# A graph attention layer's feed-forward with tanh in place of Silu, its last step on VectorE, and roots read two places later

## The chip, the cores and the metric

The kernel runs on one core of a Trainium2 chip. A core has a matrix engine (TensorE, PE in the profile), three engines for elementwise work (VectorE or DVE, ScalarE or ACT, GpSimd or POOL) and SyncE (SP), which issues DMAs. Each engine works through its own instructions in order; semaphores hold one back until another engine or a DMA has delivered. The metric is the device time of one execution in microseconds (us). The kernel before takes 10435.46 us, the median of three runs (10427.23 to 10443.66).

## The reference

Two graph layers on 10000 nodes with 512 features and 160000 edges sorted by their target node, each followed by a residual sum and a normalisation. The first layer is a mixture of four graph convolutions of two steps each, of which two are chosen per node. The second is attention along the edges with eight heads of 64, then a feed-forward part, which is what the change touches:

```
z = layernorm(x)
q, k, v = z @ Wq.T, z @ Wk.T, z @ Wv.T             (split into 8 heads)
s = sum(q[src] * k[dst]) / sqrt(64) + att_bias     (per edge and head)
alpha = softmax of s over the edges of one node
x = x + (sum of alpha * v[dst]) @ Wo.T + bo
z = layernorm(x)
x = x + silu(z @ W1.T + b1) @ W2.T + b2            (W1: 1024 x 512)
```

silu(v) is v times the logistic function of v, which equals (v/2) (1 + tanh(v/2)). The layer's own residual and one more normalisation end the computation. All data are 32-bit floats.

## The kernel before

Nodes are taken in 79 blocks of 128, and a block in four windows of 32 nodes. The edges of a window lie in up to five chunks of 128 (`CAP`). `fast` runs through four stages. First the edges are sorted into slots, interleaved with the first convolution step. The second convolution step follows, block by block, with the residual, two normalisations by `normed` (L721) and the projections to q, k and v, which go to memory. These stages are held together by TensorE's order.

The last stage is attention and feed-forward, over 316 windows. Its order on TensorE, VectorE, ScalarE and POOL is written out by hand (`manual_schedule`): each engine receives its instructions in the order in which the Python loop over `w` issues them. In each window:

- POOL gathers keys and values of the edges by indirect DMA, two windows ahead (`pull`, L1397, into four buffers `kvb`).
- TensorE turns the one-hot edge matrices (L1406), ScalarE copies them out of PSUM (L1409), and TensorE expands the queries to the edges in three groups (`expand`, L1610, into two PSUM buffers `qe`).
- VectorE multiplies expanded queries by keys, one instruction per group (`score`, L1624), and reduces over each head (L1651).
- `weigh` makes weights out of scores, in steps that are spread over three windows: per-head maxima (L1519), turned by TensorE (L1521), reduced again (`top`, L1524), spread (L1526) and subtracted (L1528); the exponential on ScalarE (L1531), with a check against very low scores (`far`, L1533); weights times one-hot matrices, in part on POOL, in part on VectorE (`ohp`, L1540); the weighted sum of the values on TensorE (`sums`, L1554); the division by the denominator (`den`, L1559 and L1560; `att`, L1563); and the turned result, copied to `att_t` (L1566).

Output projection, normalisations and feed-forward are filled in between these as jobs. A job is a Python generator: it issues instructions and yields a cost. `advance(rate)` is called four times per window, in two of them with a credit (2.6 and 2.4), and goes once through the list of jobs. A job that has yielded 0 takes one step per call; a positive cost is a step of TensorE, which is issued while the credit lasts. So a `yield 0` puts the rest of a job one place (about a quarter of a window) later.

- `front(b)`: output projection of a block (L1423), residual (L1429), statistics (L1432) and `scale`, normalised rows on ScalarE (L1435), turned (L1446) and copied to `z_t` (L1447). Two blocks share one `z_t`.
- `back`: for two blocks, the eight pieces `f` of the hidden layer. Each piece takes four products of TensorE into one half of a PSUM bank (L1464), then Silu on ScalarE, which writes `hid` (L1466). Piece f + 2 uses the same half bank as f. Then, for each block, eight down products (L1473).
- `tail`: residual (L1481), statistics (L1485), `scale`, the result `o` on ScalarE (L1488) and its store (L1490).
- `scale`: aggregate on VectorE (L1502); the root on ScalarE (L1505); one place later reciprocal and product on VectorE (L1507, L1508). Only after them is the normalised row computed.

Pools hold two buffers per name unless a tile says otherwise (`bufs`). ScalarE evaluates functions from tables; a table load (ACT_TABLE_LOAD) appears in the profile with the line of the function that needs it.

Of the kernel before, what the change touches and what calls it, by code (L numbers as in the profile page):

```python
# [8 lines left out]
F32 = mybir.dt.float32  # L9
# [3 lines left out]
AF = mybir.ActivationFunctionType  # L13
ALU = mybir.AluOpType
# [4 lines left out]
P = 128  # L19
# [6 lines left out]
HID = 1024  # L26
# [604 lines left out]
def fast(ctx: ExitStack, tc: tile.TileContext, a: dict, out: bass.AP, bad: bass.AP):  # L631
# [7 lines left out]
    nc = tc.nc  # L639
    x = a["x"]  # L640
# [39 lines left out]
    def load_cols(pool, name, ap):  # L680
        t = pool.tile([P, ap.shape[0] // P], F32, name=name)
        nc.scalar.dma_start(t, ap.rearrange("(k p) -> p k", p=P))
        return t
# [9 lines left out]
    def bias_rows(pool, vectors, folded):  # L693


        n = len(vectors)
        rows = pool.tile([P, n, D], BF16, name="rows")
        onesb = pool.tile([P, P], BF16, name="onesb")
        nc.vector.memset(rows, 0.0)
        nc.vector.memset(onesb, 1.0)  # L700
        with tc.tile_pool(name="split", bufs=1) as bp:
            full = bp.tile([3, n, D], F32, name="full")
            for i, v in enumerate(vectors):
                nc.scalar.dma_start(full[:, i, :], bass.AP(
                    tensor=v.tensor, offset=v.offset, ap=[[0, 3], [1, D]]))
            folded(full)
            part = bp.tile([3, n, D], BF16, name="part")
            mine = bp.tile([3, n, D], F32, name="mine")
            left = bp.tile([3, n, D], F32, name="left")
            nc.vector.tensor_copy(part, full)  # L710
            nc.vector.tensor_scalar(mine, part, ident[:3, 0:1], None, op0=ALU.mult)
            nc.vector.tensor_sub(left, full, part)
            for i in (1, 2):
                nc.vector.tensor_copy(part, left)
                nc.vector.scalar_tensor_tensor(mine, part, ident[:3, i:i + 1], mine,
                                               op0=ALU.mult, op1=ALU.add)
                nc.vector.tensor_sub(left, left, part)
            nc.vector.tensor_copy(rows[:3], mine)
        return rows, onesb

    def normed(pool, src, name):  # L721
        st = pool.tile([P, 6], F32, name="st")
        nc.vector.bn_stats(st, src)
        mv = pool.tile([P, 2], F32, name="mv")
        nc.vector.bn_aggr(mv, st)
        rs = pool.tile([P, 2], F32, name="rs")
        nc.scalar.activation(rs[:, 0:1], mv[:, 1:2], AF.Sqrt, bias=eps)
        nc.vector.reciprocal(rs[:, 0:1], rs[:, 0:1])
        nc.vector.scalar_tensor_tensor(rs[:, 1:2], mv[:, 0:1], -1.0, rs[:, 0:1],
                                       op0=ALU.mult, op1=ALU.mult)  # L730
        t = pool.tile([P, D], F32, name=name)
        nc.scalar.activation(t, src, AF.Identity, scale=rs[:, 0:1], bias=rs[:, 1:2])
        return t
# [11 lines left out]
    with tc.tile_pool(name="fill", bufs=1) as fp:  # L745
        FC = -(-NC // 10)
        f = fp.tile([P, FC, WP], F32, name="f")
# [8 lines left out]
    with tc.tile_pool(name="win", bufs=1) as one, tc.tile_pool(name="win2", bufs=2) as two, \  # L756
# [28 lines left out]
        for t in range(T):  # L785
# [6 lines left out]
            m = two.tile([P, C], BF16, name="m")  # L792
# [4 lines left out]
                                           op0=ALU.mult, op1=ALU.add)  # L797
# [4 lines left out]
            for dst, flat in ((d_w, flat_d), (s_w, flat_s)):  # L802
# [8 lines left out]
                                           op0=ALU.is_gt, op1=ALU.add)  # L811
# [3 lines left out]
                                           op0=ALU.mult, op1=ALU.add)  # L815
            for c in range(CAP):
                for src, to in ((loc, loc_t[t]), (idx, idx_t[t])):
# [9 lines left out]
                                op0=ALU.not_equal)  # L827
# [320 lines left out]
    with ExitStack() as p2:  # L1148
# [7 lines left out]
        def fold(full):  # L1156
# [3 lines left out]
            for i, w in enumerate(wqkv):  # L1160
# [5 lines left out]
                for k in range(KD):  # L1166
# [3 lines left out]
        bias, onesb = bias_rows(wp, [a["L0_gnn_bl"][e, 1] for e in range(NE)]  # L1170
                                + [a[f"L1_gnn_b{n}"] for n in "qkv"], fold)
        gp = p2.enter_context(tc.tile_pool(name="p2g", bufs=1))
        dp = p2.enter_context(tc.tile_pool(name="p2", bufs=2))
# [71 lines left out]
        with tc.manual_schedule(engines={ET.PE, ET.Pool}):  # L1245
# [5 lines left out]
            for b in range(NB):  # L1251
# [46 lines left out]
                for v in range(2):  # L1298
                    nc.vector.scalar_tensor_tensor(t[v], p_ag[v], inv_deg[:, b:b + 1], t[v],  # L1299
                                                   op0=ALU.mult, op1=ALU.add)  # L1300
                    nc.scalar.activation(t[v], t[v], AF.Relu, scale=gsel[:, v, b:b + 1])  # L1301
                    nc.vector.tensor_add(xb, xb, t[v])
                x1 = normed(dp, xb, "x1")
                nc.sync.dma_start(x1_all[b * P:(b + 1) * P, :], x1)
                pending = project(b, normed(dp, x1, "z"))
            drive(pending, 2)
            drive(scat, C)
# [3 lines left out]
    with ExitStack() as p3:  # L1311
# [11 lines left out]
        b1 = load_cols(wp, "b1", a["L1_gnn_b1"])  # L1323
# [3 lines left out]
        for f in range(HID // P):  # L1327
            for k in range(KD):
                nc.tensor.matmul(pb[:, f:f + 1], w1[:, k, f * P:(f + 1) * P], ln_b[:, k:k + 1],
                                 start=(k == 0), stop=(k == KD - 1))  # L1330
        nc.vector.tensor_add(b1, b1, pb[:, :HID // P])
        for k in range(KD):
            nc.vector.tensor_scalar(w1[:, k, :], w1[:, k, :], ln_g[:, k:k + 1], None, op0=ALU.mult)
        bias, onesb = bias_rows(wp, [a["L1_gnn_bo"], a["L1_gnn_b2"]], lambda full: None)
# [8 lines left out]
        dp = p3.enter_context(tc.tile_pool(name="p3", bufs=2))  # L1343
# [72 lines left out]
        def front(b):  # L1416
# [14 lines left out]
            st = dp.tile([P, 6], F32, name="st")  # L1431
            nc.vector.bn_stats(st, x2)  # L1432
            rs, mean = yield from scale(st)
            z = dp.tile([P, D], F32, name="z")
            nc.scalar.activation(z, x2, AF.Identity, scale=rs, bias=mean)  # L1435
# [14 lines left out]
            if i or b == NB - 1:  # L1450
                jobs.append(Job(back(*pairs.pop(b // 2))))

        def back(z_t, mine):

            m = P * len(mine)
            yield 0
            bank = yield from take()
            hid = dp.tile([P, HID // P, 2 * P], F32, name="hid", bufs=1)
            for f in range(HID // P):
                ph = banks[bank][:, (f % 2) * 2 * P:(f % 2) * 2 * P + m]  # L1460
                for k in range(KD):
                    if k % 2 == 0:
                        yield UP
                    nc.tensor.matmul(ph, w1[:, k, f * P:(f + 1) * P], z_t[:, k, :m],  # L1464
                                     start=(k == 0), stop=(k == KD - 1))
                nc.scalar.activation(hid[:, f, :m], ph, AF.Silu, bias=b1[:, f:f + 1])  # L1466
            unused.append(bank)
            for i, (b, x2) in enumerate(mine):
                bank = yield from take()
                po = banks[bank]  # L1470
                for k in range(HID // P):
                    yield DOWN
                    nc.tensor.matmul(po, hid[:, k, i * P:(i + 1) * P], w2[:, k, :],  # L1473
                                     start=(k == 0), stop=False)
                nc.tensor.matmul(po, onesb, bias[:, 1, :], start=False, stop=True)
                jobs.append(Job(tail(b, x2, bank)))

        def tail(b, x2, bank):
            yield 0
            yield 0  # L1480
            nc.vector.tensor_add(x2, x2, banks[bank])  # L1481
            unused.append(bank)
            yield 0
            st = dp.tile([P, 6], F32, name="st")
            nc.vector.bn_stats(st, x2)  # L1485
            rs, mean = yield from scale(st)
            o = dp.tile([P, D], F32, name="o")
            nc.scalar.activation(o, x2, AF.Identity, scale=rs, bias=mean)  # L1488
            n = min(P, N - b * P)
            nc.sync.dma_start(out[b * P:b * P + n, :], o[:n, :])  # L1490
# [3 lines left out]
        def take():  # L1494
            while not unused:
                yield 0
            return unused.pop(0)

        def scale(st):
            yield 0  # L1500
            mv = dp.tile([P, 2], F32, name="mv")
            nc.vector.bn_aggr(mv, st)  # L1502
            yield 0
            rs = dp.tile([P, 2], F32, name="rs")
            nc.scalar.activation(rs[:, 0:1], mv[:, 1:2], AF.Sqrt, bias=eps)  # L1505
            yield 0
            nc.vector.reciprocal(rs[:, 0:1], rs[:, 0:1])  # L1507
            nc.vector.scalar_tensor_tensor(rs[:, 1:2], mv[:, 0:1], -1.0, rs[:, 0:1],  # L1508
                                           op0=ALU.mult, op1=ALU.mult)
            yield 0  # L1510
            return rs[:, 0:1], rs[:, 1:2]
# [59 lines left out]
        jobs = []  # L1571
# [101 lines left out]
@with_exitstack  # L1673
def gnn_kernel(ctx: ExitStack, tc: tile.TileContext, a: dict, out: bass.AP):

    nc = tc.nc  # L1680
    with tc.tile_pool(name="flag", bufs=1) as fl:
        bad = fl.tile([P, 1], F32, name="bad")
        fast(tc, a, out, bad)
        bad_i = fl.tile([P, 1], I32, name="bad_i")
        nc.vector.tensor_copy(bad_i, bad)
        flag = nc.values_load(bad_i[0:1, 0:1])
        with tc.If(flag > 0):
            general(tc, a, out)
# [33 lines left out]
```

## Time and profile before

| what | us |
| --- | --- |
| median of three runs | 10435.46 |
| the profiled execution, its own time | 11344.71 |
| its span, first to last instruction | 11342.9 |
| busy: TensorE | 9955.5 (88% of the span) |
| busy: VectorE | 5363.8 (47%) |
| busy: ScalarE | 2940.8 (26%) |
| busy: GpSimd | 7044.1 (62%) |
| the loop over windows in the last stage | 3294, from 7958 to 11252 |
| busy in this loop: TensorE, VectorE, ScalarE | 2698, 2687, 1780 |

The profile is of one execution, which took 909 us more than the median of the runs without a profile. Busy times are unions of the spans of an engine's instructions; a table load counts as busy. The answers on the trace come in several views. The groups list instructions of one line, engine, operation and shape: count, busy time, mean duration in ns, then the idle time of the engine ahead of them and what ended it. The waits list which instruction of an engine waited for which other one. The windows give the busy time of each engine in chosen stretches. The timeline lists instructions in order of time. "issue" is idle time that no recorded event explains, "remote" a wait whose source isn't in the records.

### The profile page before, as it was taken

The numbers are of one execution on the slowest core, as the hardware profiler recorded it, in microseconds if no ns is written. First come the engines' busy times: TensorE is split into PE (matmuls) and PEld (weight loads), VectorE is DVE, ScalarE is ACT, GpSimd is POOL, SyncE is SP. The second block draws the span as 40 slices with busy tenths as digits, with TensorE's granted clock in tenths as the row PEclk, the third lists the DMA queues.
The fourth block names the chain that finished last, engine by engine and source line by source line (L and its number), as shares of the span: only waits on it lengthen the run. The fifth ranks groups of instructions, "written<-read, shape, count | busy, mean of one in ns | idle before, by whom it ended". The sixth has DMA issues, their size and how long they took to land.

```text
span 11342.9 us, 168726 instructions
## 1 busy us (share of the span) xinstructions
PE 9955.5 (88%) x63571; PEld 5699.6 (50%) x63887; DVE 5363.8 (47%) x8116; ACT 2940.8 (26%) x5400; POOL 7044.1 (62%) x6990
## 2 busy tenths in 40 slices
PE   7999989999999996898998989988788888888887
PEld 4666666666666663333333333333455555555554
DVE  5887870000000002333333333333787888888886
ACT  1111111111111110111111111111355555555554
POOL 4555656666666663666666666664666666666664
PEclk9999999999999997999999999998799999999999
DMA  6444444444444434777777777775777777777774
GB/s 207 144 139 148 145 136 145 151 139 148 133 151 148 141 123 140 244 255 257 262 256 247 256 253 257 260 245 184 225 227 225 223 231 228 228 230 228 228 228 128
DMA packets 1104625, 2252.31 MB, mean 199 GB/s; under 512 B 283935, under 2 KB 528543, under 8 KB 1103799
## 3 DMA queue, kind: packets, MB, share of 16 engines
q0 software_dynamic: 622352, 1654.70, 45.7%
q1 hardware_dynamic: 472064, 569.10, 15.3%
q10 hardware_dynamic: 9382, 17.60, 0.4%
q8 instruction: 507, 8.31, 0.3%
q14 instruction: 320, 2.61, 0.1%
HBM read 2297.25 MB, written 377.00 MB: 236 GB/s over the span
## 4 chain that ended last, share of the span: by engine, by line
PE 67%; DVE 14%; issue 8%; ACT 7%; another core or an unknown queue 3%; DMA 1%; POOL 0%; ACTq 0%; SPq 0%; DVEq 0%; POOLq 0%
PE mm L1072 16%; PE mm L1083 9%; PE mm L1275 9%; PE mm L1224 7%; PE p_ag L1262 6%; PE p_ag L1042 4%; PE bank L1464 3%; DVE kv L1624 2%; PE bank L1473 2%; PE sums L1554 2%; DVE s L1651 2%; DVE scan L894 2%; PE qe L1610 2%; ACT L1466 2%
## 5 line engine op out<-in xcount | busy, mean ns | idle before, releaser
L1015 POOL DMA_INDIRECT g<-in_x_dram,idx_t x1580 | 1873.3, 1186 | 1409.4 <-PE p_ag L1042 926.9
L1207 POOL DMA_INDIRECT y<-y_tab,ix x1580 | 1627.2, 1030 | 1022.8 <-PE p_ag L1262 421.6
L1397 POOL DMA_INDIRECT kv<-kv_all,meta x1580 | 1680.2, 1063 | 445.7 <-issue 314.0
L937 POOL DMA_INDIRECT sorted<-pay,addr x1250 | 1267.4, 1014 | 380.8 <-issue 363.7
L1275 PE MATMUL mm<-wr,hb 128*128 128x512 f32 x2528 | 1238.5, 620 | 147.8 <-issue 134.1
L1072 PE MATMUL mm<-tt,wl 128*128 128x256 f32 (+1 forms) x5120 | 1230.0, 383 | 15.6 <-issue 15.5
L1072 PE MATMUL mm<-tt,wr 128*128 128x256 f32 (+1 forms) x5120 | 1202.2, 377 | 9.9 <-issue 9.8
L1037 DVE TENSOR_SCALAR inv_deg<-small 128x1 f32<-128x1 f32 x79 | 12.5, 158 | 2447.3 <-PE small L1034 2388.5
L1083 PE MATMUL mm<-wn,h 128*128 128x512 f32 x2528 | 1127.2, 597 | 16.8 <-issue 14.9
L1624 DVE TENSOR_TENSOR kv<-qe,kv 128x1024 f32<-128x1024 f32 x948 | 972.8, 1040 | 277.8 <-PE qe L1610 230.0
L1072 PEld LDWEIGHTS mm<-tt,wl 128*128 128x128 f32 x5120 | 969.2, 193 | 241.7 <-issue 77.0
L1072 PEld LDWEIGHTS mm<-tt,wr 128*128 128x128 f32 x5120 | 967.3, 191 | 140.6 <-issue 10.6
L1074 ACT ACTIVATE h<-mm,bl 128x256 f32<-128x256 f32 (+1 forms) x640 | 297.0, 472 | 2823.8 <-PE mm L1072 1414.0
L1262 PE MATMUL p_ag<-y,oh 128*32 128x512 f32 x6320 | 835.3, 599 | 127.9 <-issue 116.0
L1651 DVE TENSOR_REDUCE s<-kv 128x40 f32<-128x2560 f32 x316 | 886.6, 2806 | 0.0
L1275 PEld LDWEIGHTS mm<-wr,hb 128*128 128x128 f32 x2528 | 483.7, 197 | 783.6 <-issue 748.4
L1464 PE MATMUL bank<-z_t,w 128*128 128x256 f32 (+1 forms) x2560 | 662.7, 401 | 224.3 <-ACT hid L1466 217.6
L1083 PEld LDWEIGHTS mm<-wn,h 128*128 128x128 f32 x2528 | 470.9, 190 | 622.0 <-issue 592.4
L1554 PE MATMUL sums<-kv,ohp 128*32 128x65 f32 x25280 | 584.4, 231 | 212.3 <-issue 209.5
L1540 POOL TENSOR_TENSOR ohp<-oh,p 128x512 f32<-128x512 bf16 x316 | 331.1, 1048 | 690.2 <-ACT p L1531 688.8
L1301 ACT ACTIVATE t<-t,gsel 128x512 f32<-128x512 f32 x158 | 109.1, 723 | 2336.2 <-DVE t L1299 1692.7
L1464 PEld LDWEIGHTS bank<-z_t,w 128*128 128x128 f32 x2560 | 488.4, 200 | 381.2 <-ACT hid L1466 279.6
(254 smaller groups left out, 12980.8 us busy)
## 6 DMA issues: line engine op xcount, KB each, us to landing
y_tab<-y SPq DMA_DIRECT2D x632, 256.0 KB
hb<-h_tab SPq DMA_DIRECT2D x316, 256.0 KB
h_tab<-h SPq DMA_DIRECT2D x156, 512.0 KB
kv_all<-kvt SPq DMA_DIRECT2D x79, 516.0 KB
xb<-in_x_dram SPq DMA_DIRECT2D x156, 256.0 KB
q_all<-q SPq DMA_DIRECT2D x79, 384.0 KB
q<-q_all SPq DMA_DIRECT2D x237, 128.0 KB
g<-in_x_dram,idx_t POOLq DMA_INDIRECT x1580
```

What stands on the lines that cost most here:

```text
L937: inst = nc.gpsimd.indirect_dma_start(out=sorted1[:], out_offset=bass.IndirectOffsetOnAxis(ap=addr_i[:, c0 + c:c0 + c + 1], axis=0), in_=p ...
L1015: nc.gpsimd.indirect_dma_start(out=gbuf[i % GB], out_offset=None, in_=x, in_offset=bass.IndirectOffsetOnAxis(ap=window(idx_t, b)[:, j, c:c ...
L1072: nc.tensor.matmul(ph[:, :n], w[:, k, f * P:(f + 1) * P], tt[:, i, k, :n], start=(i + k == 0), stop=(i == 1 and k == KD - 1))
L1083: nc.tensor.matmul(py, h[:, k, i * P:(i + 1) * P], wn[e][:, k, :], start=(k == 0), stop=(k == KD - 1))
L1207: nc.gpsimd.indirect_dma_start(out=ybuf[i % YB], out_offset=None, in_=y_flat, in_offset=bass.IndirectOffsetOnAxis(ap=ahead[b][1][:, j, c:c ...
L1262: nc.tensor.matmul(p_ag[v][j * W:(j + 1) * W, :], oh[:, j * CAP + c, :], g[:, v * D:(v + 1) * D], start=(c == 0), stop=(c == CAP - 1))
L1275: nc.tensor.matmul(pr, hb[:, k, :], wr[e][:, k, :], start=(k == 0), stop=False)
L1397: nc.gpsimd.indirect_dma_start(out=kvb[w % KB][:, c, :], out_offset=None, in_=kv_all[:], in_offset=bass.IndirectOffsetOnAxis(ap=blocks[b][ ...
L1464: nc.tensor.matmul(ph, w1[:, k, f * P:(f + 1) * P], z_t[:, k, :m], start=(k == 0), stop=(k == KD - 1))
L1554: nc.tensor.matmul(acc[h * W:(h + 1) * W, f, :], ohp[:, c, f * 4 + h, :], kv[:, c, v:v + VH], start=(c == 0 and f == 0), stop=(c == CAP - ...
L1624: nc.vector.tensor_tensor(k, qe.pop((w, g))[:, :len(cs), :], k, op=ALU.mult)
L1651: nc.vector.tensor_reduce(s, kv[:, :, :D].rearrange("p c (h d) -> p c h d", h=H), axis=AX.X, op=ALU.add)
```

## The change

Four edits, all on the normalised rows and the hidden layer.

- Silu is replaced by three instructions per piece: tanh of half the argument into a new tile `th`, half the argument itself into `hid` (Identity), both on ScalarE from PSUM, and, in a new job `gate`, (th + 1) * hid on VectorE. The bias b1 is halved once, ahead of the loop.
- `back` goes on to its down products only when all eight gates of the pair have been issued (`done`).
- In `scale` one more `yield 0` stands between the root and its reciprocal.
- `mv` and `rs`, which hold variance and root, get four buffers in place of two, in `scale` and in `normed`.

```diff
     def normed(pool, src, name):
...
-        mv = pool.tile([P, 2], F32, name="mv")
+        mv = pool.tile([P, 2], F32, name="mv", bufs=4)
...
-        rs = pool.tile([P, 2], F32, name="rs")
+        rs = pool.tile([P, 2], F32, name="rs", bufs=4)
...
         nc.vector.tensor_add(b1, b1, pb[:, :HID // P])
+        nc.vector.tensor_scalar(b1, b1, 0.5, None, op0=ALU.mult)
...
             bank = yield from take()
+            done = []
...
-                nc.scalar.activation(hid[:, f, :m], ph, AF.Silu, bias=b1[:, f:f + 1])
+
+                th = dp.tile([P, 2 * P], F32, name="th")
+                nc.scalar.activation(th[:, :m], ph, AF.Tanh, scale=0.5, bias=b1[:, f:f + 1])
+                nc.scalar.activation(hid[:, f, :m], ph, AF.Identity, scale=0.5,
+                                     bias=b1[:, f:f + 1])
+                jobs.append(Job(gate(hid[:, f, :m], th[:, :m], done)))
             unused.append(bank)
+            while len(done) < HID // P:
+                yield 0
...
+        def gate(x, th, done):
+            yield 0
+            nc.vector.scalar_tensor_tensor(x, th, 1.0, x, op0=ALU.add, op1=ALU.mult)
+            done.append(1)
...
         def scale(st):
             yield 0
-            mv = dp.tile([P, 2], F32, name="mv")
+            mv = dp.tile([P, 2], F32, name="mv", bufs=4)
...
-            rs = dp.tile([P, 2], F32, name="rs")
+            rs = dp.tile([P, 2], F32, name="rs", bufs=4)
             nc.scalar.activation(rs[:, 0:1], mv[:, 1:2], AF.Sqrt, bias=eps)
+            yield 0
             yield 0
             nc.vector.reciprocal(rs[:, 0:1], rs[:, 0:1])
```

## The prediction

> **What bounds the kernel now.** I first read the 40 slices of the page. All the instructions that the change adds or moves lie in the last stage (slices 29 to 40), and there no engine is full: PE's digit is 8, VectorE's 8 or 7, ScalarE's 5. Such a stage is held by waits between engines. Next the groups with shapes kept apart, ScalarE's:
>
> ```profile
> L1531 ACT ACT_TABLE_LOAD x231 | 296.4, 1283 | 389.9 <-DVE s L1528 253.6 <-DVE kv L1624 82.1 <-issue 54.2
> L1466 ACT ACT_TABLE_LOAD x230 | 295.1, 1283 | 5.1 <-PE bank L1464 1.1
> L1505 ACT ACT_TABLE_LOAD x156 | 200.1, 1283 | 2.3
> L1466 ACT ACTIVATE hid<-bank,b 128x256 f32<-128x256 f32 x312 | 148.1, 475 | 350.4 <-PE bank L1464 311.3 <-issue 37.6
> ```
>
> Exponential, Silu and root displace each other: 617 table loads, 792 us of ScalarE. Whether they cost time, the waits tell, over the loop of windows (7966 to 11252 us), VectorE's first, then TensorE's (total us, times, longest):
>
> ```profile
> DVE kv L1624 <- PE qe L1610: 230.0, 105, 4.4
> DVE rs L1507 <- ACT rs L1505: 132.2, 97, 4.8
> DVE x L1429 <- remote: 81.1, 74, 3.5
> ...
> PE sums L1554 <- issue: 209.5, 421, 1.2
> PE bank L1464 <- ACT hid L1466: 208.4, 145, 3.4
> PE bank L1473 <- ACT hid L1466: 55.7, 38, 1.7
> ```
>
> VectorE waits 132 us for roots, and 230 us for expanded queries from a TensorE that itself waited 264 us for `hid`. Last, one period of the order, eight windows (two blocks), cut where the reduction of L1651 starts:
>
> ```profile
> 9605.08:9618.22 13.14, 8.88 (x119) 7.02 (x122) 8.56 (x16) 8.08 (x12) 8.35 (x9) 1.00 0.74 238
> 9618.22:9628.56 10.34, 8.73 (x112) 5.40 (x102) 8.95 (x15) 6.12 (x11) 6.28 (x7) 1.00 0.57 181
> 9628.56:9639.92 11.36, 9.05 (x130) 7.13 (x134) 7.83 (x14) 8.01 (x14) 6.68 (x7) 1.00 0.90 272
> 9639.92:9649.47 9.55, 8.09 (x117) 5.37 (x105) 7.67 (x12) 5.94 (x11) 6.40 (x8) 1.00 0.48 152
> 9649.47:9659.36 9.89, 8.42 (x118) 5.04 (x115) 9.59 (x16) 4.93 (x10) 7.92 (x9) 1.00 0.78 244
> 9659.36:9669.43 10.07, 9.54 (x142) 5.62 (x142) 9.19 (x19) 3.85 (x7) 6.70 (x7) 1.00 0.79 262
> 9669.43:9677.55 8.12, 6.93 (x71) 3.56 (x69) 7.73 (x14) 4.50 (x10) 5.92 (x7) 1.00 0.78 237
> 9677.55:9687.33 9.78, 7.63 (x105) 5.04 (x107) 8.94 (x15) 4.86 (x11) 7.53 (x8) 0.83 0.73 235
> sum 82.25, PE 67.28 PEld 44.19 DVE 68.45 ACT 46.29 POOL 55.79; mean PE 8.41 PEld 5.52 DVE 8.56 ACT 5.79 POOL 6.97
> ```
>
> Columns: stretch, length, busy PE, PEld, DVE, ACT, POOL, PE's clock, DMA. I call the windows A to H. E to H are VectorE's own: it idles 0.3, 0.9, 0.4 and 0.8 us in them. A, B, C and D, in which feed-forward products and roots meet, leave it idle 4.6, 1.4, 3.5 and 1.9 us. The timeline of window C (start, duration, instruction, idle before) shows how:
>
> ```profile
> 9633.51 1.28 ACT L1505 ACT_TABLE_LOAD   x1
> 9634.81 0.30 ACT L1505 ACTIVATE rs<-mv,eps 128x1 f32<-128x1 f32 x1
> 9635.12 1.28 ACT L1466 ACT_TABLE_LOAD   x1
> ...
> 9636.95 1.99 PE L1464 MATMUL bank<-z_t,w 128*128 128x256 f32 x8 [1.70 <-ACT hid L1466]
> ```
>
> Between two Silus stand two loads and a root; TensorE needs the half bank that Silu reads, and stops.
>
> [...] no load stands between tanh and exponential. [...] in window C the root starts 1.30 us after its load does. [...] Here PE's clock is 0.94 over the loop, and the records put nearly all half-clock stretches into H and A, after thin filling and around A's long waits.
>
> **The change part by part**, against the profiled execution (11344.71 us; its loop 3294 us).
>
> Loads. In the changed order of instructions the last stage has 156 for roots, 115 ahead of exponentials and 41 ahead of tanh: 312. Gone: 305 x 1.283 = 391 us of ScalarE.
>
> Second activation (Identity, no table of its own): 320, priced by L1466's 475 ns, 152 us. ScalarE's busy time in the loop falls from 1780 to about 1540 us; it isn't the bound, but a piece f now holds its half bank for two activations, 0.95 us, which is what four products of the next piece take (0.24 us each by the timeline). That is covered while ScalarE has nothing else queued, and costs up to 0.7 us where a copy (L1409, 0.69) or att (0.52) comes between.
>
> Gates on VectorE: 312 of 128x256 and 8 of 128x128. No row has this shape; L1302 takes 696 ns for 512 columns. [...] Bounds: 111 us (348 ns, half of L1302's) to 152 us (L1299's 743 ns, PSUM and 512 columns, less 267 for 256 of them). In E to H this would show in full, but the order puts gates into A, B, C and D only, one, one, three, three.
>
> Roots and other moves. The root's result is read after the scores instead of between them, a half window later; tail steps shift with it. In C the order becomes: root load, root, load for tanh, tanh, Identity, and the gate reads these ahead of `top` (L1524). So the stall of the reciprocal becomes, once per period, a gate behind 2.9 us of loads and root and 0.95 of activations: with att done about 4.2 us into the window, hid is ready at 8.1, where VectorE wants it at about 6.6: 1.5 us. Queued behind that gate are top and two scores, for which PE's maxima and query products wait.
>
> VectorE's work by window, from the rows above with what the order adds or takes (x 0.69, statistics 0.69, aggregate 0.18, root pair 0.25, gate 0.42): A 8.56+1.73 = 10.29; B 8.95+0.67 = 9.62; C 7.83+1.27 = 9.10; D 7.67+1.27 = 8.94; E 9.59-1.38 = 8.21; F 9.19-0.43 = 8.76; G 7.73+1.56 = 9.29; H 8.94-1.31 = 7.63. Sum 71.8 us. Idle that I leave: A 0.8, B 1.3 (L1429 still waits for the output product, 1.25 in the timeline), C 1.5, D 1.0, E 0.4, F 0.8, G 0.5, H 0.6: 6.9. A period is then 78.7 instead of 82.25 us, 3.5 less; 39.5 periods: -138 us.
>
> Clock. The loop averages 83.7 us per period against 82.25 in this one: 1.4 x 39.4 = 57 us belong to half-clock stretches. A's long waits go, thin windows (0.6 us of filling) stay: half, -28 us; bounds -57 and +20.
>
> Edits at nothing, together: `back` waits for its last gates, so down products start one window later; what hides it is other filling, and the order shows the same period of eight windows, with six up products (1.4 us) more left for the end. With two late gates there, +3 us. bufs=4 for `mv` and `rs` lets two roots be under way; in the first stages no instruction changes place on any engine. The buffer of `th` (two) makes tanh f+2 wait for gate f, issued a half window earlier: free unless VectorE is behind. Halving b1 is one 128x8 operation before the loop. On SP, an output store moves past x1 or q loads; x1 is loaded some 17 us before its use (9606.45 against 9625.08), so a store that waits 3 us for `o` delays nothing. POOL's order is unchanged.
>
> Sum: -138 - 28 + 3 = -163 us; 11182 for the profiled execution. The median before is 10435.46, 909 us less than the profiled one, and the page doesn't say where the profile costs them. If the loop shrinks in proportion (0.92), -150; otherwise -163. I take -160: **10275 us**.
>
> **Rivals.**
>
> 1. The loop without the profile is nearer VectorE's bound. PE's 209 us of "issue" ahead of sums may be the profile's own. A period of 82.25 x 0.92 = 75.7 with 68.45 of VectorE has 7.2 of idling to give; 71.8 + 4.4 = 76.2 would be no gain: 10400 to 10460. Against it: loads and waits for roots are instructions, not records.
> 2. Slower: gates stall VectorE. It takes its queue in order, and 312 gates stand ahead of scores or top. I count 2.2 us of gate waits per period; if each gate waits 0.52 us more (163/312), the gain is gone; at 1 us more, +149: 10585. For it: ScalarE serves att, copies and root ahead of the second half's tanh. Against: before a gate stand 3.6 us (reduction to den) or 2.2 us (score, ohp) of VectorE's own.
> 3. More: idling in A to D falls to that of E to H (0.6): 71.8 + 4.8 = 76.6, -223, and all of the clock's 57: 10155. For it: PE needs only about 67 of 82 us.
> 4. No fewer loads: excluded by the order of the changed instructions.
>
> **How the numbers follow.** Forecast (10200 to 10350): 0.60. Rival 1: 0.15, of it 0.04 without difference and 0.03 slower. Rival 2: 0.11. Rival 3: 0.14. A change within 0.2% (21 us, about what a measurement of this kernel can tell) is 10415 to 10456. Faster: 0.60 + 0.14 + 0.08 = 0.82; same 0.04; slower 0.14. Range: below lies half of rival 3's chance, above most of rival 2's: 10140 to 10450.
>
> **What would show it.** In the groups: 312 loads, Identity near 475[...]. In the waits: L1507 on L1505 nearly gone, L1464 on ScalarE under 80 us, L1473's wait gone. In eight windows: C above 10, A near 11, the sum near 79. It is wrong if gates show long waits for ScalarE (rival 2), or if the loop in the profile shrinks by 160 us and the median does not (rival 1).

## The result and the profile after

The changed kernel is slower: 10597.83 us against 10435.71 us (medians of four runs each), a ratio of 1.0156 (95% interval 1.0138 to 1.0173), 162 us more. Forecast were 160 us less.

One thing about the base has to be said first. The same program has two levels of time: the kernel before takes some 11340 us at the upper and some 10440 us at the lower, and all runs of one session are at one level. (The expectations speak of slow and quick chips; but chip number 12 stands beside both levels on record, and what sets the level stays open.) The profile that the prediction was read from is of the upper level, the result of the lower. All ratios below are to the kernel before in the same session. Here a profile of the kernel before at the lower level (10440.89 us) is compared with that of the changed kernel (10595.55 us).

ScalarE's groups of the changed kernel, shapes apart:

```profile
L1519 ACT ACT_TABLE_LOAD x156 | 200.1, 1283 | 2.3
L1470 ACT ACTIVATE th<-bank,b 128x256 f32<-128x256 f32 x312 | 147.7, 473 | 311.1 <-PE bank L1466 308.1
L1546 ACT ACT_TABLE_LOAD x115 | 147.5, 1283 | 260.3 <-DVE rs L1522 224.7 <-DVE s L1543 35.6
L1471 ACT ACTIVATE hid<-bank,b 128x256 f32<-128x256 f32 x312 | 145.5, 466 | 0.0
...
L1470 ACT ACT_TABLE_LOAD x41 | 52.6, 1283 | 2.8 <-PE bank L1466 2.1
```

The loads are 312, and the second activation costs what was forecast. ScalarE has less to do, and that wasn't what counted. The waits in the loop of windows, first before at the lower level (7239 to 10345 us), then after (7226 to 10490 us); VectorE and TensorE, total us, times, longest:

```profile
DVE kv L1624 <- PE qe L1610: 230.8, 114, 4.4
DVE rs L1507 <- ACT rs L1505: 69.7, 114, 2.7
...
PE bank L1464 <- ACT hid L1466: 229.7, 152, 4.1
...
PE bank L1473 <- ACT hid L1466: 54.8, 38, 1.7
```

```profile
DVE hid L1489 <- ACT hid L1471: 292.9, 227, 2.6
DVE kv L1639 <- PE qe L1625: 69.3, 72, 1.4
...
PE bank L1466 <- ACT hid L1471: 323.5, 265, 2.9
```

Waits for roots are gone and those for expanded queries fell by 162 us. VectorE now waits 293 us for the gates' operands, and TensorE's waits ahead of a piece of the hidden layer rose from 230 to 324 us, although table loads hardly stand between pieces any more. The loop as one window, before and after (busy PE, PEld, DVE, ACT, POOL; then PE's clock):

```profile
7239.00:10345.00 3106.00, 2564.39 (x34095) 1677.68 (x34247) 2674.98 (x4302) 1763.25 (x3250) 2137.09 (x2277) 0.96 0.76 239
```

```profile
7226.00:10490.00 3264.00, 2697.32 (x34237) 1739.64 (x34236) 2845.93 (x4600) 1508.28 (x3249) 2196.24 (x2278) 0.92 0.73 227
...
8674.45:8684.45 10.00, 8.57 (x119) 5.81 (x117) 9.86 (x17) 5.54 (x14) 7.12 (x9) 1.00 0.80 270
8684.45:8694.35 9.90, 8.63 (x110) 5.14 (x108) 9.34 (x18) 4.50 (x9) 6.49 (x7) 1.00 0.74 247
8694.35:8708.36 14.01, 9.28 (x68) 6.94 (x70) 8.90 (x17) 8.26 (x18) 6.71 (x7) 0.85 0.70 200
8708.36:8722.00 13.64, 10.29 (x174) 7.63 (x164) 10.07 (x15) 4.91 (x13) 8.21 (x8) 0.91 0.59 180
8722.00:8730.29 8.29, 8.27 (x108) 4.61 (x106) 8.19 (x13) 3.77 (x8) 6.44 (x7) 1.00 0.52 156
8730.29:8739.25 8.96, 8.96 (x112) 5.09 (x110) 8.82 (x16) 2.38 (x8) 6.78 (x9) 1.00 0.87 277
8739.25:8748.43 9.18, 5.55 (x96) 3.85 (x94) 9.01 (x18) 3.98 (x7) 6.33 (x7) 0.82 1.01 317
8748.43:8758.69 10.26, 10.26 (x116) 5.80 (x109) 8.44 (x14) 5.31 (x11) 8.18 (x8) 0.83 0.71 233
```

The loop grew by 158 us, all but 4 of the 162. VectorE's work grew by 171 us, and its idle time stayed: 431 us (3106 less 2675) before, 418 us after. So one sort of idling was exchanged for another, at the price of the gates. TensorE's clock fell as well, from 0.96 to 0.92. The eight rows below the first are the windows A to H. Six are 8.3 to 10.3 us; C and D, with three gates each, take 14.0 and 13.6. Over the whole loop C and D take 3.2 and 3.5 us more on average than in the kernel before at this level, and A 2.8 us less. The timeline of D shows what happens in them (start, duration, engine, instruction, idle before):

```profile
8711.60 1.03 PE L1466 MATMUL bank<-z_t,w 128*128 128x256 f32 x4
...
8713.10 0.47 ACT L1471 ACTIVATE hid<-bank,b 128x256 f32<-128x256 f32 x1
...
8713.60 0.43 DVE L1489 SCALAR_TENSOR_TENSOR hid<-th,hid 128x256 f32<-128x256 f32 x1 [1.67 <-ACT hid L1471]
8713.62 1.13 PE L1466 MATMUL bank<-z_t,w 128*128 128x256 f32 x4 [0.99 <-ACT hid L1471]
...
8716.19 0.47 ACT L1471 ACTIVATE hid<-bank,b 128x256 f32<-128x256 f32 x1
...
8716.69 1.79 DVE L1489 SCALAR_TENSOR_TENSOR hid<-th,hid 128x256 f32<-128x256 f32 x1 [0.67 <-ACT hid L1471]
8716.71 1.99 PE L1466 MATMUL bank<-z_t,w 128*128 128x256 f32 x8 [0.99 <-ACT hid L1471]
...
8719.61 0.42 DVE L1489 SCALAR_TENSOR_TENSOR hid<-th,hid 128x256 f32<-128x256 f32 x1 [1.13 <-ACT hid L1471]
...
8720.30 0.39 PE L1541 MATMUL turns<-ident,top 128*128 128x8 f32 x2 [1.37 <-DVE top L1539]
```

Both later pieces start 0.05 us after the second activation of the piece before has ended (8713.57 and 8716.66). In the whole trace no piece starts sooner than that, and 279 of 319 start just then. TensorE and ScalarE work one after the other here, some 3 us per piece. VectorE stands at the gate meanwhile, and the maxima behind it (`top`) then keep TensorE waiting in its turn. The half banks were meant to let two pieces overlap, and that doesn't happen: in none of the 319 cases does TensorE write a piece while ScalarE reads the one before from the other half. (In this kernel each bank is also one tile, so the runs don't tell whether bank or tile is what holds the piece back.) The same holds in the kernel before: no piece starts sooner than 0.05 us after ScalarE's reading of the one before, and 165 of 319 start just then, as here in its window C:

```profile
8649.05 0.47 ACT L1466 ACTIVATE hid<-bank,b 128x256 f32<-128x256 f32 x1
...
8649.57 1.99 PE L1464 MATMUL bank<-z_t,w 128*128 128x256 f32 x8 [1.83 <-ACT hid L1466]
```

### The profile page after: what moved, and what is told of

Same layout as the page of the kernel before. It is cut to its first block, busy times and chain, and to the rows that moved or that the text cites. A ratio compares the mean times of both kernels' runs of the same rounds, so it can differ in the third digit from the quotient of the medians.

```text
span 10593.7 us, 169309 instructions
## 1 busy us (share of the span) xinstructions
PE 9625.3 (91%) x63887; PEld 5618.5 (53%) x63887; DVE 5534.7 (52%) x8437; ACT 2692.5 (25%) x5415; POOL 7046.9 (67%) x6990
## 4 chain that ended last, share of the span: by engine, by line
PE 63%; DVE 20%; DMA 6%; ACT 5%; issue 4%; POOL 1%; SPq 0%; ACTq 0%; DVEq 0%; POOLq 0%
PE mm L1072 17%; PE mm L1083 9%; PE mm L1275 9%; PE mm L1224 5%; PE p_ag L1262 5%; DVE s L1666 5%; DMA y<-y_tab,ix 5%; DVE kv L1639 5%; PE bank L1466 3%; PE p_ag L1042 3%; PE bank L1482 2%; DVE scan L894 2%; PE sums L1569 2%; PE qe L1625 1%; DVE m L857 1%
## 5 line engine op out<-in xcount | busy, mean ns | idle before, releaser
L1398 POOL DMA_INDIRECT kv<-kv_all,meta x1580 | 1707.6, 1081 | 446.9 <-issue 275.7
L1275 PE MATMUL mm<-wr,hb 128*128 128x512 f32 x2528 | 1144.9, 595 | 0.0
L1262 PE MATMUL p_ag<-y,oh 128*32 128x512 f32 x6320 | 813.2, 598 | 103.3 <-DMA y<-y_tab,ix 52.2
L1625 PE MATMUL qe<-q,oh_t 96*128 96x512 bf16 x1580 | 562.3, 424 | 77.6 <-DVE kv L1639 77.6
L1283 DVE SCALAR_TENSOR_TENSOR t<-mm,pick,t 128x512 f32<-128x512 f32 x474 | 334.1, 747 | 555.8 <-PE mm L1277 555.8
```

The lines of the kernel that those rows point to most:

```text
L1262: nc.tensor.matmul(p_ag[v][j * W:(j + 1) * W, :], oh[:, j * CAP + c, :], g[:, v * D:(v + 1) * D], start=(c == 0), stop=(c == CAP - 1))
L1275: nc.tensor.matmul(pr, hb[:, k, :], wr[e][:, k, :], start=(k == 0), stop=False)
L1398: nc.gpsimd.indirect_dma_start(out=kvb[w % KB][:, c, :], out_offset=None, in_=kv_all[:], in_offset=bass.IndirectOffsetOnAxis(ap=blocks[b][ ...
L1625: nc.tensor.matmul(qe[w, g][:, i, :], hots[w][:, c, :], queries[b][:, j, :], start=True, stop=True)
```

## The experiments

**The profile of before once more.** No edit; the first session was at the upper level, a later one at the lower.

> The kernel before, unchanged, profiled once more. Theory of the disturbed profile: the first profile of before was drawn out by memory traffic in all stages (its second stage took 3444 us against 2981 in the changed kernel, whose code there is the same), so this profile comes near 10440 us, its loop of windows near 3100 us in place of 3294, and VectorE idles some 10 us per eight windows in place of 13.8. Rival: profiling itself costs the kernel before 900 us, and this one shows 11300 again.

11346 us, with the profile and, in eleven runs, without it (median 11335.14). Both theories fall: the first profile was not a disturbed one, and the profile costs next to nothing. The whole session was at the upper level.

> The kernel before once more. If this chip is of the quick kind (10440 us): the theory of the disturbed profile says that TensorE's waits put down to issue, 206 us ahead of the weighted sums, are gone, and the loop of windows takes near 3110 us. On a slow chip as in the first look: 11345 us, nothing new.

10440.89 us, and the loop takes 3106 us. What differs most is in TensorE's waits in the loop; at the upper level (e0_before):

```profile
PE bank L1464 <- ACT hid L1466: 207.1, 144, 3.0
PE sums L1554 <- issue: 205.9, 416, 1.2
```

At the lower level the second wait is absent. The profile that the prediction used had it too, with 209.5 us; the level of the result doesn't. Where it comes from, no record says.

**The changed kernel at the upper level**, as a reference for its variants there.

> The changed kernel itself, beside the same runs of the kernel before as its variants. Both theories: its ratio to before is that of the result, 1.016, if the chip is of the quick kind; where memory is slower, and before waits more for gathered rows, the same waits of VectorE for gates (some 300 us) and of TensorE for ScalarE (some 325 us), and a ratio between 1.000 and 1.016.

11377.37 us, 1.0034 (1.0019 to 1.0050), with 291 us of waits for gates and 296 ahead of pieces in the loop. The change costs 49 us there and not 162: the loop of the kernel before is 173 us longer than at the lower level (3279 us), that of the changed kernel only 58 (3322 us). So what the variants below gain at the upper level is read against 1.0034, and is no direct share of the 162 us.

**The roots' edit alone.**

```diff
 (kernel before)
             nc.scalar.activation(rs[:, 0:1], mv[:, 1:2], AF.Sqrt, bias=eps)
+            yield 0
             yield 0
 (and bufs=4 for mv and rs)
```

> The kernel before with the roots' edit alone (one more place between root and reciprocal, four buffers), Silu as it was. Theory of the shared bank (the loss is the second reading of the bank by ScalarE and the gates behind it): this edit takes VectorE's waits for roots away and costs nothing, 10340 to 10430 us. Rival, the moved jobs cost the time: 10500 or more.

1.0061 (1.0035 to 1.0087), close to the rival's forecast: the gain didn't come. Waits for roots left the list, but TensorE waited 295 us ahead of pieces in the loop, not 207, and VectorE 346 us for queries, not 227. The waits moved and grew.

**Tanh alone**, the changed kernel without the roots' edit.

> The changed kernel without the roots' edit: tanh, Identity and gates alone. Theory of the shared bank: at least as slow as the changed kernel, 10590 to 10700 us. Rival, the moved jobs cost the time: 10450 or less.

1.0299 (1.0263 to 1.0335). At least as slow as the changed kernel, as expected; VectorE's waits for gates were 633 us (590 for hid, 43 for th). Each half of the change costs time; the roots' edit softens the tanh.

**The order of the two activations.**

```diff
-                nc.scalar.activation(th[:, :m], ph, AF.Tanh, scale=0.5, bias=b1[:, f:f + 1])
                 nc.scalar.activation(hid[:, f, :m], ph, AF.Identity, scale=0.5,
                                      bias=b1[:, f:f + 1])
+                nc.scalar.activation(th[:, :m], hid[:, f, :m], AF.Tanh)
```

> The changed kernel with ScalarE's two activations of a piece exchanged: Identity reads the bank first, tanh then reads Identity's result from SBUF, so that the bank is free 0.37 us earlier, while the gate's operands are ready as before. Theory of the shared bank: TensorE's waits for ScalarE before a piece fall by some 100 us (320 x 0.37), and the time by 60 to 120 us, to 10480 to 10540. Rival, the gates' place in VectorE's queue alone costs the time: less than 30 us, 10570 to 10600.

0.9961 (0.9943 to 0.9979), 0.7% below the changed kernel; waits ahead of pieces 188 us, where they had been 296. The bank is given back one activation earlier, and that takes 0.34 us of waiting off each of 320 pieces. VectorE's wait for gates is still 245 us.

**The gate one place later.**

```diff
         def gate(x, th, done):
             yield 0
+            yield 0
 (and bufs=3 for th)
```

> The changed kernel with the gate one place later (one more place in the job, three buffers of th). Theory of the early gate (VectorE meets the gate before ScalarE has delivered, and all that is queued behind it, maxima and scores, is late for TensorE): VectorE's waits for gates fall from 296 us below 80, and the time by 100 to 200 us against the changed kernel. Theory of the shared bank alone (TensorE, ScalarE and TensorE again, piece after piece, set the time; the gate's wait is where VectorE meets it): VectorE waits for TensorE's query products instead, and the time moves by less than 40 us.

1.0022 (1.0008 to 1.0037), no difference from the changed kernel (1.0034) that the intervals show, as the theory of the shared bank alone had it. The gates' wait left the list, and another took its place (loop, VectorE):

```profile
DVE kv L1640 <- PE qe L1626: 336.9, 151, 5.4
```

So while pieces share a bank, VectorE's wait at the gate is no cause by itself: VectorE meets TensorE's delay wherever it looks next.

**Without the gate's instruction.** The multiplication is left out (162 us for the 312 full gates in e7_after), both activations stay.

> The changed kernel without the gate's instruction on VectorE (the multiplication of the halved argument by tanh plus one is left out; both activations stay). Theory of the early gate: waits and 135 us of work of VectorE go, 200 to 330 us below the changed kernel. Theory of the shared bank alone: TensorE's waits before pieces stay at 300 us and more, 60 us or less below it.

0.9958 (0.9946 to 0.9970), some 0.8% (86 us) below the changed kernel, though the gates' work and waits are both gone: TensorE still waits 294 us ahead of pieces and VectorE 395 us for queries. That lies between the two forecasts, nearer to the shared bank's.

**Identity first and the gate later.**

> Both edits: Identity first from the bank and tanh from SBUF, and the gate one place later. Early gate and shared bank together: the waits of both kinds fall, 150 to 280 us below the changed kernel, below before too. If the early gate alone matters: as the late gate alone, within 30 us.

0.9854 (0.9828 to 0.9881): 1.8% below the changed kernel, more than the two edits' 0.7% and 0.1% together, and within the forecast for both causes. Each edit alone leaves the other cause in place; VectorE's waits for queries, 337 us with late gates alone, are 133 us here.

**The same with the root read one place after its issue.**

> Identity first and gate one place later, with the root read one place after its issue as in the kernel before. Theory that the roots' edit is what lets tanh be used (without it the changed kernel was 3% slower than before): 100 to 300 us above the kernel with both edits. Rival, with late gates the root's place doesn't matter: within 40 us.

0.9933 (0.9910 to 0.9956), 0.8% or some 90 us slower than with the roots' edit (0.9854, from another session), a little under the bound named. The roots' edit is worth something where gates are late.

**A bank per piece.** `take` and `unused.append` move into the loop over f.

```diff
-            bank = yield from take()
             for f in range(HID // P):
-                ph = banks[bank][:, (f % 2) * 2 * P:(f % 2) * 2 * P + m]
+                bank = yield from take()
+                ph = banks[bank][:, :m]
...
+                unused.append(bank)
-            unused.append(bank)
```

In the changed kernel, in the kernel before, and with Identity first and late gates:

> The changed kernel, in which each piece of the hidden layer takes a bank of its own from the list of two and gives it back, in place of the halves of one bank. Theory of the shared bank (a piece's first product waits until ScalarE has read the piece before, because both lie in one bank, 0.05 us after its end each time): TensorE's waits before pieces fall from 280 us below 120, VectorE's for gates with them, and the time by 80 to 200 us against the changed kernel. Rival, ScalarE's own queue makes the pieces late: less than 40 us.

> The kernel before, Silu as it was, with a bank of its own for each piece. Theory of the shared bank: it holds in the kernel before too, and part of the 207 us goes though table loads stay: 40 to 150 us below before. Rival, the loads alone make it wait: less than 30 us.

> Identity first, gate one place later, and a bank of its own for each piece. Theory of the shared bank: the 157 us of waits before pieces that are left go, 40 to 120 us below the kernel with the first two edits. Rival, VectorE is the bound by now (71.8 us of work in a period of 78.7): less than 30 us.

In the changed kernel 1.0008 (0.9988 to 1.0027), waits ahead of pieces unchanged (289 us). By the code `front` holds the other bank from the output projection to the turning, and in the trace only 2 of 319 pieces start before the reading of the one before has ended: the edit did next to nothing there, and tells nothing. In the kernel with both edits it is the same: 0.9811 (0.9773 to 0.9849), 1 of 319. In the kernel before 85 of 319 pieces do start early: 0.9913 (0.9885 to 0.9941), and the waits ahead of pieces fell from 207 to 75 us, with VectorE's and ScalarE's instructions in the same order as before. The shared bank costs time with Silu too.

**Two banks really free.** `front` gives its bank back after its sum and takes one again for the turning.

```diff
             nc.vector.tensor_add(x2, po, x1)
+            unused.append(bank)
...
+            bank = yield from take()
+            po = banks[bank]
             yield TURN
```

These three ran at the lower level, beside 10441.5 us for the kernel before. The changed kernel:

> The changed kernel with a bank of its own for each piece, and with the output projection's bank given back after its sum and taken again for the turning, so that two banks are really free while pieces run (in the changed kernel with piece banks alone the projection held the second one, so that edit did nothing). Theory of the shared bank: TensorE's waits before pieces fall from 280 us below 120, VectorE's for gates by half, and the time by 80 to 200 us against the changed kernel, a ratio to before of 0.985 to 0.997. Rival, gates and ScalarE's queue alone: within 40 us of the changed kernel, 1.000 to 1.007.

1.0070 (1.0053 to 1.0087), 0.85% (90 us) below the changed kernel. 239 of 319 pieces now start before the reading of the one before has ended, and waits ahead of pieces fell from 324 us to nothing in the list. But VectorE's waits for gates stayed (loop):

```profile
DVE hid L1492 <- ACT hid L1474: 279.8, 224, 2.3
...
PE turns L1544 <- DVE top L1542: 211.4, 155, 2.5
```

So this edit gives back about half of the 162 us. That this is the bank's share is not quite shown, since the edit also moves jobs: some 280 of VectorE's 8437 instructions stand elsewhere in its order, about 80 gates among them. What is left points to the gates' early place: TensorE, now free, waits for the maxima behind the gates. My halving of that wait was wrong. With Identity first and late gates besides:

> Identity first, gate one place later, and two banks really free for pieces. Theory of the shared bank: the waits before pieces that are left (155 us) go below 60, and 30 to 100 us with them, a ratio to before of 0.972 to 0.982. Rival, VectorE and its gates are the bound now: 0.981 to 0.988 as without.

0.9855 (0.9839 to 0.9872), and of its loop of 2979 us VectorE is busy 2814. That is 218 us below the run before it, and the rival had it: with the waits for gates gone from the list, VectorE is nearly the bound (94% busy), gates included. Last, the kernel before with two free banks:

> The kernel before, Silu as it was, with two banks really free for pieces. Theory of the shared bank: a little below the kernel before with piece banks (0.991), 0.980 to 0.991, table loads and waits for roots stay. Rival: as that one, or slower since the projection has to wait for a bank.

0.9771 (0.9755 to 0.9787), 10204.09 us: 237 us below the kernel before, more than the theory had forecast, and the best of all at that level. Its loop:

```profile
7230.00:10115.00 2885.00, 2536.53 (x34094) 1688.92 (x34246) 2673.63 (x4302) 1752.82 (x3250) 2126.30 (x2277) 0.96 0.82 257
```

It has all 617 table loads and Silu. VectorE's work is as before (2674 us), its idle time half (211 us). All but ten instructions of VectorE and ScalarE stand in the order of the kernel before, so the gain is the banks'. With two of them free, 163 of 319 pieces start before ScalarE has read the piece before; in the kernel before none did. The waits ahead of pieces, which the loads seemed to cause, are gone from the list though the loads are all there. What loads still cost with free banks no run shows by itself: the best variant with about half of them pays for that with gates (0.9855).

**Two open ends.** The roots' edit on that kernel, and the changed kernel with free banks and late gates:

> The kernel before, Silu as it was, with two banks really free for pieces (0.977 to before) and with the roots' edit. The roots alone cost 0.6%, with TensorE waiting 281 us before pieces. Theory that they cost it through the bank (the output projection held one half a window longer, and root loads came between pieces of one bank): with free banks they take VectorE's 100 us of waits for roots away, ratio 0.950 to 0.972. Rival, the moved jobs themselves cost the time: 0.980 to 0.990.

> The changed kernel with the gate one place later and two banks really free, tanh read first as in the change. Theory that the second reading of the bank costs time only through the shared bank: as fast as with Identity first, ratio to before 0.981 to 0.989. Rival, the order of the two activations matters by itself: 0.992 to 1.002.

Both ran at the upper level. The first gave 0.9802 (0.9769 to 0.9836), on the rival's side, but its partner without the edit (0.9771) ran at the lower level; whether the roots' edit helps there stays open. The second gave 0.9817 (0.9779 to 0.9855), within what was expected if the second reading costs only through the bank; with Identity first it was 0.9855 at the lower level. Beside the 1.0070 of the same kernel with early gates (lower level) it also speaks for the gates' place as a cause: waits for gates are 65 us here and were 280 there.

## Why the prediction was wrong

The step that failed is the overlap: the prediction let TensorE's next piece run under ScalarE's two activations, and let gates find their operands nearly ready. The runs show the two engines taking turns on one bank, and gates waiting 293 us.

Right: 312 loads, with none at the 265 changes between tanh and exponential; the price of Identity (466 ns in place of 475) and that of an undisturbed gate (426 ns; the profile before gave only bounds for it, 348 and 476 ns, and the 0.42 us in my sums by window was shown by none of its rows); the end of root waits; window by window, A, B, E, F and G came out 0.3 to 1.0 us below my figures on average.

Wrong, by the steps of the prediction:

1. **"Second activation", the cover.** I said that a piece holds its *half bank* for 0.95 us while four products of the next piece run. They didn't: no piece started sooner than 0.05 us after ScalarE's end, and the profile before showed as much, since none did there either. I had also misread x8 in the timeline as eight products of 0.24 us: each product leaves two records (2560 of them for 1280 instructions), so that the four products of a piece take 1.99 us. By itself that would only have lengthened the cover; in turns it is added to the activations. TensorE's waits ahead of pieces were to fall under 80 us; they rose by 94. The edit that frees two banks gives back 90 us.
2. **"Roots and other moves", the gates' waits.** I counted 2.2 us per period, one late gate in C of 1.5 us among them. Measured: 293 us in the loop, 7.4 per period. In C and D, where I had 10.6 and 9.9 us, windows take 13.8 and 13.0 on average. Rival 2 had this mechanism and its break-even at 0.52 us per gate beyond my count; the excess is 5.2 us per period or 0.65 us per gate, and it had 0.11 of the chance. But the serial bank, which rival 2 didn't name, had a part in these waits, and that its 10585 us lies so near to the measured time is in part luck, since it was reckoned from the upper level's base.
3. **The base.** A period of 82.25 us, or 83.7 on average, was that of the upper level. At the lower the kernel before takes 79.3 us per period, and the 209 us of "issue" are absent. My 78.7 us against this would have been 24 us of gain, near to rival 1, which had the profile as the reason. I knew of the 909 us between profile and median and put them down to the profile.
4. **"Gates", the size.** My bounds were 111 and 152 us; 181 were measured (312 of mean 574 ns, 8 of 293); see the last section.
5. **"Clock".** I took half of 57 us off for fewer half-clock stretches. They grew, from 229 to 485 us of the loop at the lower level, mostly in G, C, H and D, and TensorE's busy time grew by 133 us for nearly the same instructions. H, where I had 8.2 us, takes 10.1 on average, and in the period shown TensorE is busy throughout it at 0.83. Half of the 256 us more is an estimate of what this cost TensorE, 128 us; how much of it is in the 162 us no run tells apart. It went with the gates' place more than with the bank: with free banks and early gates the clock is still 0.92, with late gates and Identity first 0.96. I had also taken idling to set the half clock off, and in the loop of the profile before A and H do hold 282 of its 331 us. But that idling sets it off, no run shows; the longest idle span of TensorE in the changed kernel's loop is 2.92 us.

The sum shows the balance: VectorE's idle time of 431 us was to shrink by much more than the gates' work; it shrank by 13.

## What to carry to other kernels

When an engine waits for another's reading of PSUM, look at the bank and not at the columns: here two halves of one bank, which was also one tile, acted as one buffer. In the kernel before none of 319 pieces started ahead of the end of the reading before it; with two banks free 163 did. Count the time from the last product to the next piece's first one; if it equals the reading each time, free a bank before making the reading cheaper. And where a table load stands on a waiting path, ask whether other work can pass it, before paying with work on the fuller engine to be rid of it.

## What the runs showed of the hardware

Elementwise instructions of VectorE took longer beside one of POOL. Most gates take 0.43 us, but 32 of 320 take 1.6 us or more, and all 32 overlap POOL's sum of two tiles in `front` (L1437, 1.28 us), as in this stretch of the timeline:

```profile
7545.85 1.79 DVE L1489 SCALAR_TENSOR_TENSOR hid<-th,hid 128x256 f32<-128x256 f32 x1 [0.67 <-ACT hid L1471]
...
7546.07 1.27 POOL L1437 TENSOR_TENSOR x<-x,x 128x512 f32<-128x512 f32 x1
```

The root's product (128x1) takes 0.16 us, and 0.5 us or more in 35 of 158 cases, all of them beside that sum. In the changed kernel with two free banks no gate meets POOL's sum, and none takes more than 0.50 us. What lengthens the instructions beside the sum, no run shows.

In the changed kernel's loop TensorE's clock was halved in 81 stretches. In the 5 us ahead of each it had been busy for 61% at most, 43% at the median, and its longest idle span in the loop was 2.92 us. And the same program took 10436 and 11335 us, with TensorE's unexplained "issue" waits ahead of the weighted sums at the upper level alone.
